# A graph layer on one core: source rows transposed in eight parts of three gathered tiles, between matmul tiles

## The chip, the cores and the metric

The kernel runs on one core of a Trainium2 chip. The metric is the device time of one execution in microseconds (us), and the time before is the median of 11 executions. TensorE (PE) does matrix products into PSUM, VectorE (DVE) and ScalarE (ACT) do elementwise work, GpSimd (POOL) issues the gathers by index, and SyncE (SP) and ScalarE issue the other transfers.

## The reference

There are 12,500 nodes with 32 features and 400,000 edges, sorted by their destination. With `h = max(layernorm(x), 0)`:

```
e_feat = concatenate([h[src], h[dst], edge_attr])     # 96 features per edge
v      = relu(e_feat @ W1 + b1) @ W2 + b2             # 96 -> 64 -> 32
out    = x + maximum(segment_max(v, dst), h)          # per node, over its edges
```

Since the edges are sorted by `dst`, the maximum over a node's edges is a running maximum along the edges. The rows `h[src]` are in random order and have to be fetched one by one.

## The kernel before

**Stripes and chunks.** The edges are cut into 4 stripes (`NS`), which lie on the four groups of 32 partitions, and each stripe into 196 chunks (`NCH`) of 512 edges (`C`). A chunk therefore means 2,048 edges. The main loop (L363) takes two chunks, a *pair*, at a time, so there are 98 pairs.

**Head (L149 to L268).** The layernorm is computed in four pieces of nodes, `h` is written to DRAM for the gathers (`h_d`) and split into two parts for matrix products (`hs`). TensorE projects `h` with the destination part of `W1` in 25 rounds of one transpose and one product (L222 to L231), and the result `q` goes to DRAM. Then the *window stage* (L236 to L268) compares the destinations: each chunk has only a window of at most 32 (`W`) destinations per stripe, so `q` is needed for 32 rows only, and it works out the place in the window where each node's last edge lies (`at`).

**Two ways to the source rows.** Of the 16 blocks of 128 rows (`K`) of a chunk, 12 are fetched by GpSimd: `gather(c)` (L139) issues one indirect transfer per block into the tile `gh` of that chunk, with six such tiles. The other four blocks (`MM`) are looked up by TensorE, as *matmul tiles* (`rows_by_matmul`, L278, a generator that is advanced by `next(tiles)`): seven comparisons per chunk (L285) make one-hot rows `hot`, a product with bfloat16 `others` and 14 products with `hs` (L292, L295) sum up into a PSUM bank `pv`, in which all candidates but the wanted one are pushed far down, and a maximum by VectorE (L297) picks the row into `gm`. The first two chunks and the last have no such tiles.

**A pair.** Both kinds of rows are turned into columns by `to_features` (L321): one transpose over the 12 gathered blocks and one over the four of `gm`, into `ht`. `into_ph` (L375) sums up three products in four PSUM banks `ph`: edge attributes (`ea`), the window of `q` through a mask `of` (VectorE, L370), and the source rows. ScalarE applies the ReLU (`hid`, L389), TensorE multiplies with `W2` into two banks `pv` (L399), VectorE runs the maximum along the edges, started anew at each new destination by `pb` (scan, L404). `leave_1` and `leave_2` transpose the result, pick the last edge of each node with a one-hot `last` (L340, L350), and write the rows to DRAM (`top_d`, L357). Eight matmul tiles are set between these steps.

**What sets the order.** In the loop the orders of SyncE and TensorE are those in which the program is written. Those of VectorE, ScalarE and GpSimd are set by a planner. A gather waits until VectorE has freed a buffer (six chunks back) and for a transfer eight gathers back. `pv` has three PSUM banks, `ph` four, and `tr` one.

**End (L418 to L509).** The two result arrays and `h` are read back, the maxima are taken, `x` is added. A general path (L433) for other inputs is not taken here.

Of the kernel before, what the change touches and what calls it, by code (L numbers as in the profile page):

```python
# [20 lines left out]
DVE = mybir.EngineType.DVE  # L21

# [21 lines left out]
MMC = range(2, NCH - 1)  # L44
AHEAD = 2
PIECE = 2 * A0
ROUND = 12582912.0
# [11 lines left out]
def gnn_kernel(ctx, tc, x, src, src_mm, src_t, dst, dst_next, dst_ext, lo, hi, edge_attr, weights, w1, w2, b2, out):  # L59
# [23 lines left out]
    gathered = ctx.enter_context(tc.tile_pool(name="gathered", bufs=6))  # L83
# [17 lines left out]
    lo_i = const.tile([1, NS, NCH], I32, name="lo_i")  # L101
    nc.sync.dma_start(lo_i, lo.rearrange("(o s) c -> o s c", o=1))
# [6 lines left out]
    node = const.tile([P, NCH], F32, name="node")  # L109
    for s in range(NS):  # L110
        nc.gpsimd.iota(node[s * W:(s + 1) * W], pattern=[[0, NCH]], base=0, channel_multiplier=1,
                       allow_small_or_imprecise_dtypes=True)
# [26 lines left out]
    def gather(c):  # L139
        gh = gathered.tile([P, K, D], F32, name="gh")  # L140
        for k in range(K - MM * (c in MMC)):
            if c * C + k * D < SE:
                nc.gpsimd.indirect_dma_start(  # L143
                    out=gh[:, k, :], out_offset=None, in_=h_d[:, :],
                    in_offset=bass.IndirectOffsetOnAxis(ap=src_i[:, c, k:k + 1], axis=0))
        return gh


    with tc.tile_pool(name="nodes", bufs=1) as pool, tc.tile_pool(name="nodes_ps", bufs=2, space=PSUM) as ps:  # L149
# [4 lines left out]
        sts = [pool.tile([P, 2, PIECE], F32, name=f"st{k}") for k in range(len(pieces))]  # L154
        with tc.manual_schedule(engines={DVE, SP}):
            for st, r in zip(sts, pieces):
                n = r.stop - r.start
                nc.vector.tensor_reduce(st[:, 0, :n], xs[:, r], axis=AX.X, op=ALU.add)
                nc.vector.tensor_scalar(st[:, 0, :n], st[:, 0, :n], 1.0 / D, None, op0=ALU.mult)
                nc.vector.tensor_tensor(h[:, r], xs[:, r], st[:, 0, :n, None].to_broadcast([P, n, D]),  # L160
                                        op=ALU.subtract)
                nc.scalar.activation(sq[:, r], h[:, r], AF.Square)
            for st, r in zip(sts, pieces):
                n = r.stop - r.start
                nc.vector.tensor_reduce(st[:, 1, :n], sq[:, r], axis=AX.X, op=ALU.add)
                nc.vector.tensor_scalar(st[:, 1, :n], st[:, 1, :n], 1.0 / D, EPS, op0=ALU.mult, op1=ALU.add)
                nc.scalar.activation(st[:, 0, :n], st[:, 1, :n], AF.Sqrt)
            for st, r in zip(sts, pieces):
                n = r.stop - r.start
                nc.vector.reciprocal(st[:, 1, :n], st[:, 0, :n])  # L170
                nc.vector.scalar_tensor_tensor(h[:, r], h[:, r], 0.0,
                                               st[:, 1, :n, None].to_broadcast([P, n, D]),
                                               op0=ALU.max, op1=ALU.mult)
                nc.sync.dma_start(h_v[:, r], h[:, r])
# [15 lines left out]


# [3 lines left out]
            for k in range(0, EP // P, EP // P // 4):  # L195
# [5 lines left out]
        iota_a = pool.tile([P, D, A0], F32, name="iota_a")  # L201
        nc.gpsimd.iota(iota_a, pattern=[[0, D], [1, A0]], base=0, channel_multiplier=0,
                       allow_small_or_imprecise_dtypes=True)
        nc.vector.tensor_scalar(others, iota_a, place, -LOW, op0=ALU.not_equal, op1=ALU.mult)
# [7 lines left out]
        lo_w = pool.tile([P, NCH], I32, name="lo_w")  # L212
        nc.scalar.dma_start(lo_w, ap(lo, 0, [[NCH, NS], [0, W], [1, NCH]]))
        nc.vector.tensor_tensor(node, node, lo_w, op=ALU.add)
# [7 lines left out]
        for t in range(0, NT, 4):  # L222
            n = min(4, NT - t)
            hp = ps.tile([P, P], F32, name="hp")
            nc.tensor.transpose(hp[:n * D], h[:, t:t + n].rearrange("p t f -> p (t f)"), ident)
            ht = pool.tile([P, P], F32, name="ht", bufs=2)
            nc.vector.tensor_copy(ht[:n * D], hp[:n * D])
            pp = ps.tile([P, 4, HID], F32, name="pp")
            nc.tensor.matmul(pp[:, :n].rearrange("p t o -> p (t o)"), ht[:n * D],
                             wq[:n * D, :n * HID], start=True, stop=True)  # L230
            nc.scalar.activation(qs[:, t:t + n], pp[:, :n], AF.Copy)  # L231
# [40 lines left out]
    with tc.tile_pool(name="edges", bufs=3) as pool, tc.tile_pool(name="edges_ps", bufs=1, space=PSUM) as ps, \  # L272
            tc.manual_schedule(engines={SP, PE}):
        loaded = {}
        windows = {}
        mm_rows = {}

        def rows_by_matmul():  # L278

            for i, c in enumerate(MMC):  # L280
                kb = pool.tile([P, 2, MM * P], F16, name="kb", bufs=2)
                nc.scalar.dma_start(kb, ap(key_d, i * MM * P, [[0, P], [len(MMC) * MM * P, 2], [1, MM * P]]))
                hot = pool.tile([P, A1, MM * P], F32R, name="hot", bufs=2)
                for k in range(A1):
                    nc.vector.tensor_scalar(hot[:, k], kb[:, 0], key_p[:, k:k + 1], None, op0=ALU.is_equal)  # L285
                its = pool.tile([P, MM * P], BF16, name="its", bufs=2)
                nc.vector.tensor_scalar(its, kb[:, 1], place, None, op0=ALU.is_equal)  # L287
                gm = mm_rows[c] = pool.tile([P, MM, D], F32, name="gm", bufs=6)
                for m in range(MM):
                    e = slice(m * P, (m + 1) * P)  # L290
                    po = ps.tile([P, C], F32, name="pv", bufs=3)[:, :D * A0]
                    nc.tensor.matmul(po, its[:, e], others.rearrange("p f a -> p (f a)"), start=True, stop=False)  # L292
                    for k in range(A1):
                        for part in range(2):
                            nc.tensor.matmul(po, hot[:, k, e], hs[:, part, k].rearrange("p f a -> p (f a)"),  # L295
                                             start=False, stop=(k == A1 - 1 and part == 1))
                    nc.vector.tensor_reduce(gm[:, m, :], po.rearrange("p (f a) -> p f a", a=A0),  # L297
                                            axis=AX.X, op=ALU.max)
                    yield

        def load(c):
            if c % LOAD == 0:
# [5 lines left out]
                for s in range(NS):  # L308
                    g = slice(s * D, (s + 1) * D)
                    nc.scalar.dma_start(db[g, :n], ap(dst_ext, 1 + s * S + c * C, [[0, D], [1, n]]))  # L310
                    nc.scalar.dma_start(pb[g, :n], ap(pen_d, s * S + c * C, [[0, D], [1, n]]))
                for k in range(c, min(c + LOAD, NCH)):
                    loaded[k] = [t[:, (k - c) * C:(k - c + 1) * C] for t in (ea, db, pb)]
            _, base = nc.values_load_multi_w_load_instructions(
                lo_i[0:1, :, c], engines=[SP], min_val=0, max_val=N)
            qw = pool.tile([P, HID], F32, name="qw", bufs=6)
            for s in range(NS):
                nc.sync.dma_start(qw[s * W:(s + 1) * W, :], q_d[bass.ds(base[s], W), :])
            windows[c] = qw, base

        def to_features(c, gh):  # L321
            ht = pool.tile([P, K, D], F32, name="ht", bufs=4)
            n = min(K - MM * (c in MMC), (SE - c * C) // D)
            nc.vector.transpose(ht[:, :n].rearrange("p k e -> p (k e)"), gh[:, :n].rearrange("p k f -> p (k f)"))  # L324
            if c in MMC:
                nc.vector.transpose(ht[:, n:].rearrange("p k e -> p (k e)"),
                                    mm_rows.pop(c).rearrange("p k f -> p (k f)"))
            elif n < K:
                nc.vector.memset(ht[:, n:], 0.0)
            return ht.rearrange("p k e -> p (k e)")  # L330

        def leave_1(c, sm):

            px = ps.tile([P, J, P], F32, name="tr")
            for j in range(J):
# [3 lines left out]
            last = pool.tile([P, J, NS, W], F32, name="last", bufs=2)  # L339
            nc.vector.tensor_tensor(  # L340
                last, iota_w[:, None, None, :].to_broadcast([P, J, NS, W]),
                at[:, :, c * J:(c + 1) * J].rearrange("p s j -> p j s")[:, :, :, None].to_broadcast([P, J, NS, W]),
                op=ALU.is_equal)
            return so, last

        def leave_2(c, so, last):

            pw = ps.tile([P, J, P], F32, name="tr")[:, 0]
            for j in range(J):
                nc.tensor.matmul(pw, last[:, j].rearrange("p s w -> p (s w)"), so[:, j, :],  # L350
                                 start=(j == 0), stop=(j == J - 1))
            wo = pool.tile([P, P], F32, name="wo")
            nc.scalar.activation(wo, pw, AF.Copy)  # L353
            _, base = windows.pop(c)
            for s in range(NS):
                g = slice(s * W, (s + 1) * W)
                nc.sync.dma_start(top_d[s % 2][bass.ds(base[s], W), :], wo[g, s * D:(s + 1) * D])  # L357

        tiles = rows_by_matmul()
# [211 lines left out]
```

## Time and profile before

| | |
|---|---|
| median of 11 executions | 5317.55 us (5302.12 to 5334.65) |
| profiled execution | 5313.9 us |
| its span, first to last instruction | 5312.1 us |
| mean granted TensorE clock | 0.81 |
| TensorE matmuls busy | 3656.1 us, 69% |
| TensorE weight loads busy | 2827.6 us, 53% |
| GpSimd busy | 2233.7 us, 42% |
| VectorE busy | 1846.9 us, 35% |
| ScalarE busy | 315.1 us, 6% |
| gathers (L143) | 2353, of 0.948 us each, with 0.30 us between two |
| matmul tiles | 772 |

The page gives busy times of each engine, then 40 equal slices of the span with a digit for the busy tenths, the granted clock and the transfers. Its rows of waits say which instruction waited for what, with total, number and longest in us. "issue" is time for which the profile shows no cause, "remote" a release that it can't place. In an order of time each line begins with start and length in us; the bracket holds the idle time before, and its releaser. An answer by stretches gives busy us of each engine in each. A matmul of two 32-bit operands appears as two records.

### The profile page before, as it was taken

To read this page: it belongs to the slowest core of one execution; us is meant where nothing else is said; L and a number is where in the kernel's file an instruction comes from. 1 tells how busy PE (TensorE), PEld (TensorE's weight loads), DVE (VectorE), ACT (ScalarE), POOL (GpSimd) and SP (SyncE) were. 2 spreads that over 40 slices of the span, in tenths; PEclk is the share of its full clock that TensorE was granted. 3 is DMA by queue.
4 is the path that set the end of the run, shared out by engine and by line. 5 is a ranking of instruction groups with operands and counts; after the bars stand their busy time and mean duration, and the time that the engine had idled before them with its cause. 6 is when DMAs were issued, how large, how long until landed. Compare 5 with 4: busy or idle time off the path is not lost. (4 is left out here: it accounts for less than half of the span.)

```text
span 5312.1 us, 57318 instructions
## 1 busy us (share of the span) xinstructions
PE 3656.1 (69%) x20281; PEld 2827.6 (53%) x20281; DVE 1846.9 (35%) x3612; ACT 315.1 (6%) x627; POOL 2233.7 (42%) x2369
## 2 busy tenths in 40 slices
PE   2376767676767676767676767676767676767687
PEld 1155555554555555555455555554555565555565
DVE  2333333333323232333333333333333333333344
ACT  1000000000000000000000000000000000000000
POOL 6534343434343434343444344434343434344420
PEclk6588788888888787878887878788888788878788
DMA  3321112111211121112111211121112111211121
GB/s 122 84 61 42 41 38 56 43 41 38 57 42 41 38 57 42 41 38 57 42 42 38 57 42 41 38 57 42 41 40 55 42 41 38 57 42 41 38 54 64
DMA packets 235577, 256.47 MB, mean 48 GB/s; under 512 B 123653, under 2 KB 211861, under 8 KB 222102
## 3 DMA queue, kind: packets, MB, share of 16 engines
q10 hardware_dynamic: 74084, 137.60, 9.6%
q0 software_dynamic: 75296, 38.70, 5.0%
q1 hardware_dynamic: 85906, 76.48, 4.8%
q8 instruction: 159, 2.61, 0.2%
q14 instruction: 132, 1.08, 0.1%
HBM read 238.44 MB, written 14.04 MB: 48 GB/s over the span
## 5 line engine op out<-in xcount | busy, mean ns | idle before, releaser
L143 POOL DMA_INDIRECT gh<-h_d,src_i x2353 | 2229.6, 948 | 2903.3 <-DVE ht L324 2189.4
L295 PE MATMUL pv<-hs,hot 128*128 128x448 f32 x10808 | 2868.9, 419 | 324.5 <-issue 323.8
L295 PEld LDWEIGHTS pv<-hs,hot 128*128 128x128 f32 x10808 | 2336.1, 217 | 1244.5 <-issue 1054.0
L297 DVE TENSOR_REDUCE gm<-pv 128x32 f32<-128x448 f32 x772 | 481.0, 623 | 2348.7 <-remote 1322.4
L292 PE MATMUL pv<-others,its 128*128 128x448 bf16 x772 | 307.5, 398 | 670.6 <-issue 544.1
L350 PE MATMUL tr<-so,last 128*128 128x128 f32 x1568 | 275.5, 287 | 434.0 <-issue 429.2
L285 DVE TENSOR_SCALAR hot<-kb,key_p 128x512 fp32r<-128x512 f16 x1351 | 555.7, 478 | 16.4 <-DMA qw<-q_d 16.4
L404 DVE TENSOR_TENSOR_SCAN sm<-pb,sm,pv 128x512 f32<-128x512 bf16 x195 | 248.6, 1275 | 659.0 <-remote 617.1
L350 PEld LDWEIGHTS tr<-so,last 128*128 128x128 f32 x1568 | 241.1, 201 | 405.3 <-issue 393.1
L292 PEld LDWEIGHTS <-its 128*128 128x128 bf16 x772 | 76.5, 99 | 427.9 <-issue 407.7
L389 ACT ACTIVATE hid<-ph,wt 128x512 f32<-128x512 f32 x392 | 238.7, 690 | 969.8 <-PE ph L379 476.0
L353 ACT ACTIVATE wo<-tr 128x128 f32<-128x128 f32 x196 | 54.5, 278 | 3899.3 <-remote 1213.6
L336 PE MATMUL tr<-ident,sm 128*128 128x128 f32 x784 | 131.3, 294 | 36.0 <-ACT wo L353 35.9
L338 DVE TENSOR_TENSOR so<-tr,wt 128x512 f32<-128x512 f32 x196 | 134.3, 685 | 39.4 <-PE pv L292 25.2
L336 PEld LDWEIGHTS tr<-ident,sm 128*128 128x128 f32 x784 | 104.1, 153 | 73.1 <-ACT wo L353 57.7
L340 DVE TENSOR_TENSOR last<-iota_w,at 128x512 f32<-128x512 f32 x196 | 131.5, 671 | 27.2 <-PE tr L350 27.2
L287 DVE TENSOR_SCALAR its<-kb,place 128x512 bf16<-128x512 f16 x193 | 69.9, 362 | 181.8 <-remote 167.0
L379 PE MATMUL ph<-ht,wt 32*64 32x512 f32 x1568 | 115.7, 614 | 11.4 <-issue 11.4
L324 DVE STREAM_TRANSPOSE ht<-gh 128x384 f32<-128x384 f32 (+1 forms) x196 | 102.8, 563 | 54.8 <-PE ph L379 54.8
L379 PE MATMUL ph<-ea,wt 32*64 32x512 f32 x1568 | 110.1, 617 | 8.7 <-DMA db<-in_dst_ext 8.7
L379 PE MATMUL ph<-of,qw 32*64 32x512 f32 x1568 | 105.5, 592 | 6.6 <-issue 6.6
L399 PE MATMUL pv<-hid,wt 64*32 64x512 f32 x1568 | 108.4, 601 | 0.2 <-ACT hid L389 0.2
(68 smaller groups left out, 396.1 us busy)
## 6 DMA issues: line engine op xcount, KB each, us to landing
ea<-in_edge_attr SPq DMA_DIRECT2D x49, 1024.0 KB
db<-in_dst_ext ACTq DMA_DIRECT2D x196, 256.0 KB
kb<-key_d ACTq DMA_DIRECT2D x193, 256.0 KB
gh<-h_d,src_i POOLq DMA_INDIRECT x2353
pb<-pen_d ACTq DMA_DIRECT2D x196, 128.0 KB
qw<-q_d SPq DMA_DIRECT2D x784, 8.0 KB
top_d<-wo SPq DMA_DIRECT2D x784, 4.0 KB
top_d<-zero ACTq DMA_DIRECT2D x2, 1568.0 KB
```

What stands on the lines that cost most here:

```text
L143: nc.gpsimd.indirect_dma_start(out=gh[:, k, :], out_offset=None, in_=h_d[:, :], in_offset=bass.IndirectOffsetOnAxis(ap=src_i[:, c, k:k + 1 ...
L285: nc.vector.tensor_scalar(hot[:, k], kb[:, 0], key_p[:, k:k + 1], None, op0=ALU.is_equal)
L292: nc.tensor.matmul(po, its[:, e], others.rearrange("p f a -> p (f a)"), start=True, stop=False)
L295: nc.tensor.matmul(po, hot[:, k, e], hs[:, part, k].rearrange("p f a -> p (f a)"), start=False, stop=(k == A1 - 1 and part == 1))
L297: nc.vector.tensor_reduce(gm[:, m, :], po.rearrange("p (f a) -> p f a", a=A0), axis=AX.X, op=ALU.max)
L336: nc.tensor.transpose(px[:, j, :], sm[:, j * P:(j + 1) * P], ident)
L338: nc.vector.tensor_tensor(so, px, b2r[:, None, :].to_broadcast([P, J, P]), op=ALU.add)
L340: nc.vector.tensor_tensor(last, iota_w[:, None, None, :].to_broadcast([P, J, NS, W]), at[:, :, c * J:(c + 1) * J].rearrange("p s j -> p j ...
L350: nc.tensor.matmul(pw, last[:, j].rearrange("p s w -> p (s w)"), so[:, j, :], start=(j == 0), stop=(j == J - 1))
L379: nc.tensor.matmul(ph[s][x * HID:(x + 1) * HID], w[g], e[g], start=start, stop=stop)
L389: nc.scalar.activation(hid[s], ph[s], AF.Relu, bias=b1c)
L404: nc.vector.tensor_tensor_scan(sm, loaded.pop(c + x)[2], pv[x], before, op0=ALU.add, op1=ALU.max)
```

## The change

The source rows of a pair are now transposed one pair ahead, in eight parts. `gather` fills tiles of three blocks (`SOME`), with 24 such buffers instead of six of whole chunks. `to_features(c, part)` transposes one of them right behind the matmul tile of the same number, so that one iteration transposes the eight parts of the *next* pair while it finishes its own.

The orders of VectorE and ScalarE in the loop are written out by hand too. The one-hot comparisons and the `last` masks are placed between the tiles. The mask `of` moves from VectorE (one comparison) to ScalarE (two activations, `window_hots`). All chunks but the last have matmul tiles; those of the first two stand ahead of the loop. Windows and edge data are loaded four chunks ahead instead of two. Keys come for two chunks in one transfer, `db` and `pb` for all stripes in one. The edge and window products of the next pair are issued in this iteration. `pv` has two banks; the freed one holds the numbers 0 to 31 (`iota_ps`) for the `last` masks. `leave_2` uses products of 64 columns instead of 128.

In the head, one of the four pieces of the layernorm goes to GpSimd, some small operations are merged, and the projection works on four transposes and two products at a time. In the end, `h` is put together from `hs` by GpSimd instead of being read from DRAM.

```diff
-MMC = range(2, NCH - 1)
-AHEAD = 2
+MMC = range(NCH - 1)
+SOME = 3
+AHEAD = 4
...
-    gathered = ctx.enter_context(tc.tile_pool(name="gathered", bufs=6))
+    gathered = ctx.enter_context(tc.tile_pool(name="gathered", bufs=24))
...
     def gather(c):
-        gh = gathered.tile([P, K, D], F32, name="gh")
-        for k in range(K - MM * (c in MMC)):
-            if c * C + k * D < SE:
+        n = min(K - MM * (c in MMC), (SE - c * C) // D)
+        parts = []
+        for k in range(0, n, SOME):
+            parts.append(gathered.tile([P, SOME, D], F32, name="gh"))
+            for i in range(min(SOME, n - k)):
                 nc.gpsimd.indirect_dma_start(
...
-        for t in range(0, NT, 4):
+        for t in range(0, NT, 16):
+            fours = [(k, min(4, NT - k)) for k in range(t, min(t + 16, NT), 4)]
...
-            tc.manual_schedule(engines={SP, PE}):
+            tc.manual_schedule(engines={SP, PE, DVE, ACT}):
...
+        iota_ps = ps.tile([P, C], F32, name="iota_ps")[:, :W]
+        nc.vector.tensor_copy(iota_ps, iota_w)
...
-                    po = ps.tile([P, C], F32, name="pv", bufs=3)[:, :D * A0]
+            po = ps.tile([P, C], F32, name="pv", bufs=2)[:, :D * A0]
...
+        def window_hots(c):
+            of = ofs[c] = pool.tile([P, C], F32, name="of", bufs=3)
+            nc.scalar.activation(of, loaded[c][1], AF.Square, bias=below[:, c:c + 1])
+            nc.scalar.activation(of, of, AF.Relu, bias=ones, scale=-1.0)
+
+        def to_features(c, part):
...
+            if part < J:
+                r = slice(part * SOME, min((part + 1) * SOME, n))
+                if r.start < n:
+                    nc.vector.transpose(ht[:, r].rearrange("p k e -> p (k e)"),
+                                        gh[c][part][:, :r.stop - r.start].rearrange("p k f -> p (k f)"))
+            elif c in MMC:
...
+                for g in range(2):
+                    nc.tensor.matmul(pw[g * 2 * W:(g + 1) * 2 * W],
+                                     last[:, j, 2 * g:2 * g + 2].rearrange("p s w -> p (s w)"),
+                                     so[:, j, g * 2 * D:(g + 1) * 2 * D], start=(j == 0), stop=(j == J - 1))
...
         for c in range(0, NCH, 2):
+            a, b = c + 2, c + 3
+            for k in range(a, min(a + 2, NCH)):
+                gh[k] = gather(k)
+            load_keys(a + 2)
             for k in range(c + AHEAD, min(c + AHEAD + 2, NCH)):
                 load(k)
...
+            tile(a, 0)
+            to_features(a, 0)
+            ht = [hts.pop(c + x).rearrange("p k e -> p (k e)") for x in range(2)]
+            into_ph(ph, [(w1a, ht[x]) for x in range(2)], False, True)
...
+            one_hots(b, range(3))
+            tile(a, 1)
+            to_features(a, 1)
+            one_hots(b, range(3, A1))
+            last = [lasts(c)]
+            tile(a, 2)
+            to_features(a, 2)
+            ph = edges_into(a)
...
+            windows_into(a, ph)
+            leave()
...
+            tile(a, 3)
+            to_features(a, 3)
+            to_features(a, J)
+            so = leave_1(c, sms[0])
+            last.append(lasts(c + 1))
+            tile(b, 0)
+            to_features(b, 0)
+            one_hots(a + 2, range(4))
+            leave_2(c, so, last[0])
+            tile(b, 1)
+            to_features(b, 1)
+            so = leave_1(c + 1, sms[1])
+            one_hots(a + 2, range(4, A1))
+            tile(b, 2)
+            to_features(b, 2)
+            tile(b, 3)
+            to_features(b, 3)
+            to_features(b, J)
...
-        for r in pieces:
-            nc.sync.dma_start(h[:, r], h_v[:, r])
```

In it, `tile(c, m)` is one matmul tile with its reduction, `one_hots(c, groups)` some of the seven comparisons of a chunk, and `lasts(c)` the mask of last edges.

## The prediction

> **What bounds the kernel now.** I read the page's totals and slices first, then the waits, then a table of stretches, then the order of time within one pair of chunks.
>
> ```profile
> PE 3656.1 (69%) x20281; PEld 2827.6 (53%) x20281; DVE 1846.9 (35%) x3612; ACT 315.1 (6%) x627; POOL 2233.7 (42%) x2369
> PE   2376767676767676767676767676767676767687
> POOL 6534343434343434343444344434343434344420
> PEclk6588788888888787878887878788888788878788
> ```
>
> No engine is busy throughout, yet all slices look alike until the last one and a half, where POOL (the gathers) has ended and PE and its clock rise. The waits name the partners:
>
> ```profile
> POOL gh L143 <- DVE ht L324: 2189.4, 94, 32.9
> DVE gm L297 <- remote: 1322.4, 88, 28.4
> DVE sm L404 <- remote: 617.1, 85, 13.4
> ```
>
> POOL waits once per pair for the big transposes (94 times, some 23 us), then gathers in one burst. VectorE waits some 15 + 7 us per pair for something that the profile can't name ("remote"). By the program it can only be TensorE: both instructions wait on TensorE's semaphore and for no late DMA. Four stretches of one pair each (columns: length, then busy us and count of PE, PEld, DVE, ACT, POOL, then clock, DMA share, GB/s):
>
> ```profile
> 2602.00:2655.00 53.00, 35.56 (x206) 27.86 (x205) 18.42 (x37) 3.26 (x7) 22.69 (x24) 0.82 0.27 70
> 5108.00:5152.00 44.00, 35.31 (x212) 28.70 (x211) 18.30 (x36) 2.98 (x6) 16.08 (x17) 0.92 0.11 22
> 5152.00:5184.00 32.00, 32.00 (x214) 26.10 (x213) 18.14 (x36) 2.98 (x6) 0.00 (x0) 1.00 0.25 70
> ```
>
> This decides my reading. The same work takes 53 us beside 24 gathers, 44 us beside 17, and 32 us beside none (from one first edge matmul at 5153.26 to the next at 5184.42: 31.2 us). So 31.2 us is TensorE's own time and 52.9 us is what it takes (starts at 2612.80, 2665.54, 2718.59). Inside the pair:
>
> ```profile
> 2620.03 0.94 POOL L143 DMA_INDIRECT gh<-h_d,src_i  x1 [23.37 <-DVE ht L324]
> 2625.55 1.09 PE L399 MATMUL pv<-hid,wt 64*32 64x512 f32 x16
> 2635.73 1.28 DVE L404 TENSOR_TENSOR_SCAN sm<-pb,sm,pv 128x512 f32<-128x512 bf16 x1 [7.84 <-remote]
> 2649.76 0.37 PE L350 MATMUL tr<-so,last 128*128 128x128 f32 x1 [1.73 <-issue]
> 2654.02 0.62 DVE L297 TENSOR_REDUCE gm<-pv 128x32 f32<-128x448 f32 x1 [12.98 <-remote]
> ```
>
> The burst starts at 2620.03 and, at 24 x 1.25 us, ends at 2650.3. The matmuls recorded from 2625.55 to 2626.64 are consumed only at 2635.73; between 2642 and 2653 TensorE issues one instruction per 0.7 or 1.4 us; the reduction of the tile recorded at 2626.6 to 2629.7 starts at 2654.02. A matmul's recorded end cannot be trusted here: the Trainium skill, "Perfetto Trace Analysis", section "Tensor Engine Instruction (MATMUL, LD_WEIGHTS)", says that it is estimated from the size, not observed. So I read completions from who consumes them. In the head, under a burst of 80 gathers, the pace is bare:
>
> ```profile
> 77.27 1.19 PE L229 MATMUL pp<-wt,ht 128*128 128x256 f32 x2 [6.30 <-issue]
> 85.67 1.19 PE L229 MATMUL pp<-wt,ht 128*128 128x256 f32 x2 [7.00 <-issue]
> 94.07 1.19 PE L229 MATMUL pp<-wt,ht 128*128 128x256 f32 x2 [7.00 <-issue]
> ```
>
> 8.40 us a round for three matmul and three load records: 1.40 us an instruction, against 0.11 in a free tile (30 instructions in some 3.3 us). So: a long run of gathers makes TensorE crawl. Onset: the tile before the burst's sixth us is reduced on time (2625.75), so I put it 8.5 us after the start. End: after the last gather, some 1.8 us later (tile issue resumes near 2652).
>
> Here a rule speaks against the change. The Trainium skill, "SBUF — State Buffer", section "SBUF: two separate sides", says that only the port pair shared by VectorE and GpSimd contends and that TensorE never waits on anyone. By it the 21.7 us per pair would not come from gathers, spreading them would be worth nothing, and only head and end would gain: about 5312 - 110 = 5200 us. The 53/44/32 rows say otherwise, and I go by them; what the shared path is, no row here shows.
>
> **The change, part by part.**
>
> Gathers. The number per chunk stays 12 (16 in the first two before), each with the same transfer of 128 rows. Before, two transposes free two buffers together and POOL runs 24 gathers in one go. After, each of eight transposes per pair frees a three-gather buffer, behind its own matmul tile; 24 buffers are again three pairs ahead, so landing stays hidden. Three gathers are 3.75 us; TensorE's starts of tiles in a free pair are 4.2, 3.0, 6.9 (four small groups between), 3.7, 3.9, 3.7, 3.0, 3.0 us apart, sum 31.3. So at TensorE's own pace POOL, with 30.0 us, would hardly ever pause, and the crawl would still begin; but the crawl now stops the releases, and POOL runs dry after at most a few gathers. The pair finds its own period. I take a filling store: it fills in 8.5 us of gathering, empties in 1.8 us after. If emptying goes on at one rate r and gathers fill at p, then 8.5(p - r) = 1.8r, r = 0.83p, and 24 gathers can pass in 30.0/0.83 = 36.4 us. With 0.6 us for uneven release: **37 us a pair** (estimate). Bounds: 31.2 (never sets in) and 52.9 (no help), and beyond it if it sets in at every group (below).
>
> VectorE. Two transposes of 0.56 us become eight of 96 columns: rows of 384 (0.563) and 128 columns (0.304) give 0.175 + 0.0010 a column, 0.27 each, so +1.05 us; the two compares of L370 (0.44 apart) leave: -0.88. Sum 18.3 us of 37; if that cover is gone, +0.2 us a pair, 16 us in all. Its order is now by hand: behind each reduction stand a transpose, compares, then the scans. Gather time is touched: beside the compares of L285 a gather took 1.24 instead of 0.95 us (198.72 to 203.31); 5.7 us of compares now meet gathers, some five of them, +1.4 us for POOL; within the range's upper part.
>
> ScalarE. Four activations for the window masks (nearest row: hid, 0.690): +2.8 us on 3.0, hidden under 37. They stand ahead of the next window matmuls but follow hid with two tiles (6 us) of cover. If not covered: 270 us. Key loads fall from two to one per pair, db and pb from eight to two per four chunks: some 2 us of queue less, on an idle queue. SyncE issues the same 8 window loads (6.3 us) and 8 stores (7.5 us) plus one register load for two: 14 of 37 us, and the loads start two chunks earlier.
>
> TensorE. The leaving matmuls become eight of 64 columns instead of four of 128, twice the records: between 0.5 and 1.9 us against 0.97 a time; I keep 0.97 (column halves can overlap as in L399, 16 records in 1.02 us); the worst is +1.9 us a pair, 175 us. With two tile banks instead of three, the tile after the scan waits for it: last product, then scan 1.28 us, covered by window (0.99) and leaving matmuls (0.97). Zero; without that cover 1.3 us a pair, 120 us.
>
> Head. Before, the projection rounds crawl until 121, the window stage begins at 131.9 and takes 31.4 us, and the first tile is out only at 232.3. After, projections go in fours: 25 groups at the free pace of 0.84 us (pairs at 37.35, 39.04, 40.72) end at about 43 from 22, near the onset; I allow one crawling round of 24 instructions x 1.4 = 34, so 77. Window stage to about 110, loads behind; the first burst is 72 gathers, 30 to 120. Tiles start at about 125 (bounds 110 and 200). Two chunks more by matmul: 8 tiles x 3.4 = 27. Gathers of the layernorm piece on POOL cost some us before the burst, absorbed there.
>
> End. From the last tile to the end 48.6 us; without reading h again (it lands at 5304.46, last): 45.
>
> Sum: 125 + 27 + 93.5 pairs x 37 (3459) + 3 gather-free pairs x 31.2 (94) + 45 = **3750 us**, against the profiled 5313.9 (span 5312.1); that execution lies 0.07% under the median 5317.55, which I ignore.
>
> **Rivals.** Fixed part 291 us, plus 93.5 times the period.
> - Crawl never sets in: short groups with the 6.9 us tile step clear it. 31.3 to 33 us: 3215 to 3375. For it: the first 8 us of a burst are free. Against: POOL would be 96% busy.
> - Crawl sets in after every third group and ends only when POOL pauses: fast for 11.3 us, then about 4 lost: 31.3 x 15.4/11.3 = 42.7, 4280 us; up to 50 if a cold clock (0.50 in the stalls now) adds.
> - No gain: TensorE loses 0.9 us per gather however they are placed: 52 us, 5150. For it: total gathers are equal. Against: 17 gathers lose 12.8 and 24 lose 21.7, so the first 6 or 7 are free.
> - Slower: the store does not empty in the gaps, and each three-gather group stalls TensorE. Place: between a transpose and the next tile. It decides above (5317 - 291)/93.5 = 53.8, that is 2.8 us a group; at the full 3.75 a group: 61 us, 6000. Against: a stalled TensorE gives POOL no new buffers.
>
> **How the numbers follow.** Chances: 34 to 40 us, my forecast, 0.41 (3470 to 4030); never sets in 0.22; 40 to 50 us 0.24; no gain 0.04; slower 0.09. The 8-in-10 range takes the first rival nearly whole and the second to 47 us: 3240 to 4690. Faster 0.90, same 0.01, slower 0.09, where 0.2% is what a measurement of this kernel can tell.
>
> **What would show it.** Right: pair starts about 37 us apart; gathers in threes with pauses; "remote" waits of the reductions down from 1322 to a few hundred; clock above 0.9; first tiles near 125. Wrong: period 31 with POOL without pause (no store at all); period near 53 with short pauses and crawling TensorE; VectorE or POOL without pause as bound.

## The result, and the profile after

| | before | after |
|---|---|---|
| median | 5318.09 us (31 executions, 5293.62 to 5334.65) | 4112.35 us (8 executions, 4100.2 to 4121.15) |
| profiled execution, span | 5313.9, 5312.1 us | 4126.7, 4124.9 us |
| mean granted TensorE clock | 0.81 | 0.89 |

The ratio is 0.7733, 95% interval 0.7721 to 0.7744. The forecast was 3750 us with a range of 3240 to 4690: the direction and the range held, the number was 362 us too low.

The page of the changed kernel, its totals and three rows of slices:

```profile
PE 3639.4 (88%) x21969; PEld 2509.5 (61%) x21969; DVE 1819.7 (44%) x3999; ACT 590.2 (14%) x1007; POOL 2335.6 (57%) x2377
...
PE   2699898999989998889999998999988989998996
...
POOL 7555565655555555555655556555555555655541
PEclk7789898989898899899898989898899889988998
```

TensorE's digits rise from six and seven tenths to eight and nine, and the clock is up. But this isn't work alone: without a crawl (see the experiments) the page of the same kernel has the same 21,969 matmul records busy for 3039.9 us, 600 us less. GpSimd's busy time is what it was (2336 against 2234 us), now in a span that is 1187 us shorter. The waits (total us, times, longest):

```profile
DVE gm L359 <- remote: 1207.3, 208, 20.3
...
POOL gh L148 <- DVE ht L400: 504.4, 187, 8.4
POOL gh L148 <- DVE ht L403: 481.6, 94, 9.5
```

GpSimd's wait for transposes is down from 2189 to 986 us, in three pieces a pair instead of one (281 in all, 3.5 us in the mean). The releases that the profile can't place stay: 1207 us where I had forecast a few hundred. One pair in order of time (start, length, then the idle time before and its releaser):

```profile
2016.13 1.01 POOL L148 DMA_INDIRECT gh<-h_d,src_i  x1 [3.29 <-DVE ht L400]
...
2027.82 0.95 POOL L148 DMA_INDIRECT gh<-h_d,src_i  x1 [4.31 <-DVE ht L403]
...
2037.89 0.95 POOL L148 DMA_INDIRECT gh<-h_d,src_i  x1 [2.57 <-DVE ht L400]
...
2043.76 0.62 DVE L359 TENSOR_REDUCE gm<-pv 128x32 f32<-128x448 f32 x1 [2.01 <-PE pv L356]
...
2052.07 0.95 POOL L148 DMA_INDIRECT gh<-h_d,src_i  x1 [0.30 <-issue]
...
2055.18 0.62 DVE L359 TENSOR_REDUCE gm<-pv 128x32 f32<-128x448 f32 x1 [9.24 <-remote]
...
2056.26 1.01 POOL L148 DMA_INDIRECT gh<-h_d,src_i  x1 [3.24 <-DVE ht L400]
```

Between the first and the last of these lines lie 40.13 us and 24 gathers: six, a pause of 4.31, six, a pause of 2.57, twelve, a pause of 3.24. In the long run TensorE's tiles come out on time until 2043.76, 5.9 us after its start, and then none for 11.4 us. The next is out 2.2 us after the last gather has ended (2053.02). This is the crawl of the prediction, still there, but cut short by GpSimd running dry. From 300 to 3900 us nearly all runs of gathers are of six (173) or twelve (80). A stretch of this pair, and one after the last gather (length, then busy us and count of PE, PEld, DVE, ACT, POOL, then clock, DMA share, GB/s):

```profile
2016.13:2056.26 40.13, 38.64 (x241) 25.38 (x226) 18.03 (x41) 8.00 (x14) 23.60 (x25) 0.92 0.36 82
4000.00:4032.00 32.00, 32.00 (x232) 25.37 (x231) 17.66 (x40) 5.55 (x10) 0.00 (x0) 1.00 0.32 84
```

From the first to the last edge product of a pair that runs beside gathers (158.05 to 4008.80) there are 95 pairs, 40.5 us each in the mean (by these products they alternate between some 37 and 44 us); the two after them take 30.79 us each. The pair therefore went from 52.9 to 40.5 us, and 95 x 12.4 = 1178 of the 1187 us lie there. Which part of the change saved them no run shows; the trace shows only that one wait of 23 us has become three short ones.

### The profile page after: what moved, and what is told of

Same layout as the page of the kernel before. It is cut to its first block, busy times and chain, and to the rows that moved or that the text cites. A ratio compares the mean times of both kernels' runs of the same rounds, so it can differ in the third digit from the quotient of the medians.

```text
span 4124.9 us, 59504 instructions
## 1 busy us (share of the span) xinstructions
PE 3639.4 (88%) x21969; PEld 2509.5 (61%) x21969; DVE 1819.7 (44%) x3999; ACT 590.2 (14%) x1007; POOL 2335.6 (57%) x2377
## 5 line engine op out<-in xcount | busy, mean ns | idle before, releaser
L356 PE MATMUL pv<-hs,hot 128*128 128x448 f32 x10920 | 2585.0, 385 | 179.1 <-issue 175.5
L356 PEld LDWEIGHTS pv<-hs,hot 128*128 128x128 f32 x10920 | 2101.8, 194 | 473.4 <-issue 325.6
L444 PE MATMUL ph<-ea,wt 32*64 32x512 f32 x1568 | 282.3, 921 | 65.5 <-issue 61.0
L506 PE MATMUL pv<-hid,wt 64*32 64x512 f32 x1568 | 295.3, 932 | 21.7 <-DVE last L410 12.5
L430 PEld LDWEIGHTS tr<-so,last 128*64 128x64 f32 x3136 | 128.6, 153 | 200.8 <-issue 195.8
L400 DVE STREAM_TRANSPOSE ht<-gh 128x96 f32<-128x96 f32 x782 | 209.3, 268 | 0.0
L430 PE MATMUL tr<-so,last 128*64 128x64 f32 x3136 | 165.7, 246 | 44.5 <-issue 41.2
L386 ACT ACTIVATE of<-db,below 128x512 f32<-128x512 int32 x196 | 139.2, 710 | 66.6 <-issue 66.6
L387 ACT ACTIVATE of<-of,ones 128x512 f32<-128x512 f32 x196 | 141.5, 722 | 6.4
L410 DVE TENSOR_TENSOR last<-iota_ps,at 128x512 f32<-128x512 f32 x196 | 133.0, 678 | 0.0
```

The costliest lines, as they stand in the source:

```text
L387: nc.scalar.activation(of, of, AF.Relu, bias=ones, scale=-1.0)
L400: nc.vector.transpose(ht[:, r].rearrange("p k e -> p (k e)"), gh[c][part][:, :r.stop - r.start].rearrange("p k f -> p (k f)"))
L430: nc.tensor.matmul(pw[g * 2 * W:(g + 1) * 2 * W], last[:, j, 2 * g:2 * g + 2].rearrange("p s w -> p (s w)"), so[:, j, g * 2 * D:(g + 1) * ...
L444: nc.tensor.matmul(ph[s][x * HID:(x + 1) * HID], w[g], e[g], start=start, stop=stop)
L506: nc.tensor.matmul(pv[x][s * D:(s + 1) * D], w2x[g], hid[s][g], start=True, stop=True)
```

## The experiments

**A condition that the prediction did not have in view.** The twelve runs fell on four chips. On every one of them the kernel before, run beside, took 3190.0 to 3196.2 us instead of 5294 to 5335. So a time below is compared with about 3193 us, and first comes what the trace of the unchanged kernel shows there.

**The kernel before and the changed kernel, unchanged.**

> The kernel before, unchanged, for its trace on a chip of these experiments. Theory A (gathers alone make TensorE crawl, whatever the chip): 5310 us, pairs 52.9 us apart, the reductions of matmul tiles waiting some 1300 us for a release that the trace can't place. Theory B (the crawl needs a condition of the chip beside the gathers, which this chip lacks): about 3194 us, pairs 31.2 to 31.6 us apart, no such waits, no stretch with 1.4 us a TensorE instruction, though the 24 gathers of a pair still go in one burst of 30 us.

> The changed kernel, as it is. In the last runs the kernel before took 3193.67 us instead of 5318, so there the gathers did not make TensorE crawl. If the crawl belongs to the chip or its condition: where the kernel before takes about 3190 us the change is worth little, POOL's 31.3 us and TensorE's 30.5 us a pair give 3150 to 3300 us; where the kernel before takes about 5318 us, this one takes 4112 us again. If the kernel before had only been placed better by chance in those runs and the gain is the change's own: 0.77 of the time of the kernel before in either case.

Measured: 3195.63 us for the kernel before (one execution), and 3156.8 us for the changed kernel, ratio 0.9884 (0.9855 to 0.9912). First the page, the waits and one pair of the kernel before, each a view of its own:

```profile
PE 3056.2 (96%) x20281; PEld 2469.6 (77%) x20281; DVE 1855.2 (58%) x3612; ACT 316.4 (10%) x627; POOL 2349.4 (74%) x2369
...
POOL 5777777777777777777777777777777777777750
PEclk8699999999999999999999999999999999999997
```

```profile
DVE gm L297 <- PE pv L295: 909.3, 611, 4.1
POOL gh L143 <- issue: 646.2, 2120, 0.3
```

```profile
1006.62:1037.78 31.16, 31.16 (x210) 25.32 (x209) 18.43 (x36) 2.98 (x6) 23.84 (x25) 1.00 0.18 34
```

The totals of the changed kernel, and one of its pairs:

```profile
PE 3039.9 (96%) x21969; PEld 2383.2 (75%) x21969; DVE 1826.2 (58%) x3999; ACT 563.2 (18%) x1007; POOL 2329.9 (74%) x2377
```

```profile
2016.91:2047.77 30.86, 30.86 (x225) 24.21 (x225) 17.80 (x40) 5.54 (x10) 23.54 (x25) 1.00 0.31 67
```

The gathers come 0.30 us apart, as before, and never pause; most take 0.94 us, and the mean is 0.997 instead of 0.948 us. TensorE is busy for all of a pair beside them, at clock 1.00, and no release is unplaced. So gathers alone, 24 in 31 us, don't make TensorE crawl; something that the recorded comparison had and these four chips lack is needed as well. It also turns one reading of mine round. The wait of 23 us per pair for the two big transposes was no property of buffers of whole chunks: with the same buffers and no crawl it is gone. So in the recorded comparison it was the crawl that held the transposes back.

Two candidates for the further condition can be looked at in these traces. A lower granted clock explains too little: the pair of 40.13 us had 0.92, so even if all its work went with the clock, 40.13 x 0.92 = 36.9 us would be left at full clock (an estimate), not 30.86; and from 2044 to 2055 us, while no tile came out, the granted clock was 1.00. The gathers' transfers took no longer either. Their queue in the kernel before, in the recorded comparison and here (packets, 32 for each of 2353 gathers; MB; share of the span of 16 engines):

```profile
q0 software_dynamic: 75296, 38.70, 5.0%
```

```profile
q0 software_dynamic: 75296, 38.70, 9.0%
```

That is 266 us of 5312 and 287 us of 3194.

**No gathers.** Only the first two chunks are gathered, and all others use these rows again.

```diff
+    kept = {}
+
     def gather(c):
-        gh = gathered.tile([P, K, D], F32, name="gh")
+        if c > 1:
+            return kept[c % 2]
+        kept[c] = gh = gathered.tile([P, K, D], F32, name="gh")
```

> Leaves out all gathers but those of the first two chunks, whose rows every later pair uses again, so the values are not the reference's. If the gathers make TensorE crawl: the pair falls from 52.9 us to the 31.2 us seen where none were running; 98 x 31.2 = 3058 us, with head and end 3200 to 3350 us. If the 21.7 us per pair come from the order of the work or from waits between the engines (the gathers only happen to be there): about 5200 to 5300 us.

> The changed kernel with the same left out, so again the values are not the reference's. If the gathers are all that holds it above TensorE's own time: 31 us a pair, 3100 to 3250 us. If its order by hand or its two tile banks cost something of their own (windows of VectorE or ScalarE in the way): a period of 34 to 40 us, 3450 to 4100 us.

Measured: 3176.86 us, ratio 0.9947 (0.9925 to 0.9970) for the kernel before, and 3155.6, ratio 0.9884 (0.9851 to 0.9917), for the changed one. TensorE's own time a pair is thus shown: 31.15 and 30.86 us. Compared with the runs that gather, all gathers together cost 17 us in the kernel before, and nothing that shows in the changed one (3155.6 against 3156.8 us, each from two executions that differ by more than 7).

**A slower stream of gathers.** GpSimd fills 384 columns after each gather.

```diff
                 nc.gpsimd.indirect_dma_start(
...
+                nc.gpsimd.memset(pace, 0.0)
...
-            tc.manual_schedule(engines={SP, PE}):
+            tc.manual_schedule(engines={SP, PE, POOL}):
```

(In the changed kernel POOL is added to its own list.)

> The kernel before with one small fill of 384 columns on GpSimd behind every gather, nothing left out. By its nearest rows (784 columns 0.74 us, 128 columns 0.20 us) a fill takes 0.40 us; up to 0.30 of it can lie in the pause between two gathers, so gathers come every 1.35 to 1.65 us instead of 1.25. By the filling store (it can take a gather per 1.51 us): at 1.51 us or slower TensorE doesn't crawl, a pair takes the 36 to 40 us of GpSimd, 3750 to 4150 us in all, so that slower gathers make a faster kernel; at 1.35 us the crawl comes later in the burst, 46 to 51 us a pair, 4750 to 5200 us. If each gather takes a fixed time from TensorE, or if what counts is that GpSimd is at work at all: 5300 us or more.

> The changed kernel with the same fills, nothing left out. By the filling store: at 1.51 us or slower between gathers no crawl is left, and the pair takes GpSimd's 36 to 40 us, 3750 to 4100 us; at 1.35 us 38 to 40 us a pair, 3900 to 4110 us. If each gather costs TensorE a fixed time, or GpSimd's work as such: 40.3 us a pair plus what the fills add, 4110 to 4500 us.

Measured: 3893.04 us, ratio 1.2194 (1.2158 to 1.2229), and 3818.65 us, ratio 1.1961 (1.1926 to 1.1996). Two lines from the order of time and one of the waits of the paced kernel before:

```profile
2000.02 0.95 POOL L146 DMA_INDIRECT gh<-h_d,src_i  x1 [0.17 <-issue]
2000.96 0.44 POOL L149 MEMSET pace<- 128x384 f32 x1
2001.57 0.95 POOL L146 DMA_INDIRECT gh<-h_d,src_i  x1 [0.16 <-issue]
```

```profile
DVE ht L328 <- DMA gh<-h_d,src_i: 971.1, 98, 17.6
```

A gather comes every 1.55 us instead of 1.25, and VectorE waits for rows to land: GpSimd is the bound. A time between 3800 and 3900 us here says nothing of a filling store, since there was no crawl to relieve. But the runs measure slack. In the kernel before the last gather ends 709.6 us later than without the fills (3801.6 instead of 3092.0), and the span grows by 700.5 us (3194 to 3894). In the changed one it ends 707.1 us later (3768.9 instead of 3061.9), and the span grows by 658.0 us (3159 to 3817). So GpSimd was some 9 us from being the bound before, and is some 49 us from it after.

**All eight transposes together**, behind the first tile of the pair.

```diff
             tile(a, 0)
-            to_features(a, 0)
+            for m in range(MM):
+                to_features(a, m)
+            for m in range(MM):
+                to_features(b, m)
...
             tile(a, 1)
-            to_features(a, 1)
```

(The other six calls are taken out likewise.)

> The changed kernel with only the spreading undone: the eight transposes of a pair stand together behind its first matmul tile, so that GpSimd gathers 24 blocks in one burst again; buffers of three blocks, orders by hand and everything else stay. Where the crawl exists: if the spreading is what gained, 50 to 53 us a pair, 4950 to 5250 us; if the rest of the change gained, about 4112 us. Where it doesn't exist (the kernel before at 3190 us): 3150 to 3350 us either way, as the burst of 30 us fits into the pair of 31 us.

> The changed kernel with all eight transposes of gathered rows behind the first tile of the pair, so that 24 gathers go in one burst, once more, for a chip on which the kernel before takes 5318 us. There, by the prediction (spreading is what saves), 4950 to 5250 us against 4112; if the spreading is worth nothing and another part saves, about 4112. On a chip where the kernel before takes 3194 us: 3160 us, as the first time.

Measured: 3160.6 us, ratio 0.9896 (0.9867 to 0.9924), and on another chip 3159.03, ratio 0.9891 (0.9871 to 0.9911). That is 2 to 4 us above the changed kernel's 3156.8, less than its two executions differ (3153.14 and 3160.46): where nothing crawls, the places of the eight parts are worth nothing that shows. Whether they are what saves where TensorE crawls stays open: neither run met it, and without the crawl GpSimd had no pause that a burst could follow.

**Five matmul tiles, eleven gathers.**

```diff
-MM = 4
+MM = 5
...
-                mm_rows[c] = pool.tile([P, MM, D], F32, name="gm", bufs=6)
+                mm_rows[c] = pool.tile([P, MM, D], F32, name="gm", bufs=4)
...
-                hid.append(pool.tile([P, C], F32, name="hid", bufs=6))
+                hid.append(pool.tile([P, C], F32, name="hid", bufs=4))
...
             to_features(a, 3)
+            tile(a, 4)
             to_features(a, J)
```

(The second chunk of a pair gets its fifth tile likewise. The buffers of `gm` and `hid` are fewer to make room.)

> Five matmul tiles and eleven gathers a chunk instead of four and twelve, in the changed kernel. The disputed cost is that of a tile by itself: at 3.2 us of TensorE each, two more a pair make 30.9 + 6.4 = 37.3 us, 98 pairs plus 133 us of head and end: 3790 us where nothing crawls, with GpSimd waiting (22 x 1.25 = 27.5 us of 37.3). Where TensorE crawls (the kernel before at 5318 us), 22 gathers could pass in 33 us by the filling store of the prediction, so that the pair would be TensorE's 37.3 us, 3900 us and faster than 4112; by the third-group rival two fewer gathers only take two of 24 parts of the 9.5 us lost, 37.3 + 8.7 = 46 us, 4700 us.

Measured: 3792.03 us, ratio 1.1873 (1.1849 to 1.1897), pairs 37.3 us apart. A tile costs 3.22 us of TensorE, and GpSimd now waits (view of waits):

```profile
POOL gh L148 <- DVE ht L400: 1044.6, 539, 4.4
```

With three tiles, by these prices, GpSimd would need at least 26 x 1.25 = 32.5 us a pair, more than the 30.86 that a pair takes now; that wasn't run. By this estimate four and twelve is the best split.

**The leaving matmuls.** Of the 128x128 result of a leaving time only the four diagonal blocks are read, one per stripe. Three edits: in the changed kernel back to 128 columns; on to 32; and 64 columns in the kernel before, alone. (The sizes of `wo` and its slices follow.)

```diff
-            pw = ps.tile([P, J, P], F32, name="tr")[:, 0, :2 * D]
+            pw = ps.tile([P, J, P], F32, name="tr")[:, 0]
...
-                for g in range(2):
-                    nc.tensor.matmul(pw[g * 2 * W:(g + 1) * 2 * W],
-                                     last[:, j, 2 * g:2 * g + 2].rearrange("p s w -> p (s w)"),
-                                     so[:, j, g * 2 * D:(g + 1) * 2 * D], start=(j == 0), stop=(j == J - 1))
+                nc.tensor.matmul(pw, last[:, j].rearrange("p s w -> p (s w)"), so[:, j, :],
+                                 start=(j == 0), stop=(j == J - 1))
...
```

> In the changed kernel the leaving matmuls are again four of 128 columns instead of eight of 64. If these small products are what makes a pair of the changed kernel shorter (30.86 against 31.16 us, where nothing crawls), the time rises by 98 x 0.30 = 29 us, 0.9%, to 3186 us. If both forms cost the same (the prediction's 0.97 us a time), nothing changes: 3157 us.

```diff
-                for g in range(2):
-                    nc.tensor.matmul(pw[g * 2 * W:(g + 1) * 2 * W],
-                                     last[:, j, 2 * g:2 * g + 2].rearrange("p s w -> p (s w)"),
-                                     so[:, j, g * 2 * D:(g + 1) * 2 * D], start=(j == 0), stop=(j == J - 1))
+                for g in range(NS):
+                    nc.tensor.matmul(pw[g * W:(g + 1) * W], last[:, j, g],
+                                     so[:, j, g * D:(g + 1) * D], start=(j == 0), stop=(j == J - 1))
...
```

> The changed kernel with leaving matmuls of 32 columns, one per stripe, sixteen instead of eight. If the four column quarters overlap as the two halves do, a leaving time falls from 0.62 us to 0.4 to 0.5 us and the time by 98 x 2 x 0.17 = 33 us to 3124 us (ratio 0.978 to the kernel before); if TensorE's issue of 32 records sets it, 0.6 to 1.2 us a time, 3157 to 3270 us. Where TensorE crawls at 1.4 us an instruction, 16 more records a time make a crawling pair longer: above 4112 us.

The third edit puts the loop over two halves into the kernel before, the first diff read backwards.

> The kernel before with one part of the change alone: leaving matmuls of 64 columns instead of 128. Where nothing crawls (the kernel before at about 3194 us), TensorE is busy nearly all the time, and the twice two leaving matmuls of a pair cost 0.27 us less each (0.88 to 0.62 us in the traces of e9 and e5). If that is what the change is worth there, the time falls by 98 x 0.54 = 53 us to 3141 us, ratio 0.983, and is below the changed kernel's 3157. If the gain of 37 us comes from the new order and the eight parts, the time stays at 3194 us. Where TensorE crawls (the kernel before at 5318 us), within 1% of it by the prediction's reading.

Measured: 3210.55 us with whole columns, ratio 1.0052 (1.0035 to 1.0068); 3122.02 us with quarters, ratio 0.9778 (0.9762 to 0.9794); and 3208.22 us for halves alone in the kernel before, ratio 1.0050 (1.0033 to 1.0066). In the views of groups these products are, with whole columns, halves (the changed kernel) and quarters (count, then busy us in all, mean ns of one):

```profile
L429 PE MATMUL tr<-so,last 128*128 128x128 f32 x1568 | 217.0, 282 | 3.2 <-DVE so L422 3.2
```

```profile
L430 PE MATMUL tr<-so,last 128*64 128x64 f32 x3136 | 134.8, 228 | 3.3 <-DVE so L422 3.3
```

```profile
L430 PE MATMUL tr<-so,last 128*32 128x32 f32 x6272 | 96.4, 200 | 3.3 <-DVE so L422 3.3
```

Twice the records cost less time. Each is half as wide, and they overlap: 3136 records of 228 ns are 715 us in sum and fill 134.8. A leaving time takes 0.89 to 1.00, 0.62 and 0.39 to 0.52 us, from the first record to the next work. The pair is 31.40, 30.86 and 30.46 us, the whole kernel 54 us faster by halves and 35 more by quarters. Whole columns came out above both expectations: without this part the changed kernel is 0.5% slower than the kernel before where nothing crawls. The new order costs TensorE some 0.25 us a pair (31.40 against 31.15). Of that, 0.18 is seen: edge and window products that follow each other directly take 0.91 and 0.99 us (starts at 2003.53, 2004.44, 2005.43 in the kernel before), and 1.04 each when the products with `W2` stand between them. Half of the leaving times are also longer, 1.00 instead of 0.89 us.

The halves alone missed their expectation: 3208 instead of 3141. Most pairs are as short as expected, 30.73 us, but 28 pairs past the first take 31.1 to 36.4. The longest, in order of time:

```profile
2371.09 0.94 POOL L143 DMA_INDIRECT gh<-h_d,src_i  x1 [0.30 <-issue]
2372.34 0.94 POOL L143 DMA_INDIRECT gh<-h_d,src_i  x1 [0.30 <-issue]
...
2372.89 0.58 DVE L324 STREAM_TRANSPOSE ht<-gh 128x384 f32<-128x384 f32 x1 [8.71 <-DMA gh<-h_d,src_i]
...
2374.04 1.19 PE L401 MATMUL pv<-hid,wt 64*32 64x512 f32 x14 [3.10 <-DVE gm L297]
```

and the gathers in its view of groups (busy us, mean ns, then idle time before and its releasers):

```profile
L143 POOL DMA_INDIRECT gh<-h_d,src_i x2353 | 2362.6, 1004 | 741.9 <-issue 657.7 <-DMA gh<-h_d,src_i 43.6 <-DMA h_d<-h 25.0
```

GpSimd doesn't pause: busy and idle fill the 3104 us up to its last gather, and its idle time is that between two gathers. It had some 9 us of slack and was asked for 53. With a gather every 1.309 us in the mean, 24 take 31.4 us, and that is the mean of the pairs. When GpSimd has fallen behind, VectorE waits 8.7 us at the transpose of a whole chunk for its rows to land, the reductions stand behind it, and TensorE waits 3.1 us for a bank. That the kernel is slower than before, and not only no faster, goes with longer gathers: 1.004 us in the mean instead of 0.997, so that the last one ends at 3109.4 instead of 3092.0 us. In the changed kernel the gathers, at 0.982 us beside VectorE's new order, fit. So of the 1.2% neither part does it alone: the halves free TensorE, and the rest of the change leaves GpSimd the room to follow. Which part of that rest it is wasn't tried; the places of the eight transposes are not it, by the run with all of them together. The quarters take 35 of the 49 us that were left, and are the fastest version there, 2.2% below the kernel before. They weren't run where TensorE crawls.

## Why the prediction was right or wrong

**TensorE's own time, 31.2 us a pair.** Right: 31.15 without gathers, and 31.15 beside them where nothing crawls.

**"A long run of gathers makes TensorE crawl."** This step failed as a general statement and held for the recorded comparison. The 53/44/32 us rows were a true reading of that trace, and the traces after carry on: pairs of 40.5 us beside gathers and 30.8 without. But the same 24 gathers leave TensorE at 31.15 us in the trace from one of the four chips, and the times on the other three are the same. I had weighed the rule of the Trainium skill, "SBUF — State Buffer", section "SBUF: two separate sides", that TensorE never waits on anyone. Its 5200 us was wrong for the recorded comparison by 1088 us. In that other trace the measurement agrees with it: TensorE busy for 31.16 of 31.16 us. What the further condition is, no run here shows. In the traces with a crawl, and only there, there are also releases that the profile can't place; whether that is a cause, a sign or a trait of how these executions were recorded wasn't tried.

**Onset 8.5 us, end 1.8 us.** In the pair shown, the last tile on time is out 5.9 us after the start of the run, and the next one, recorded from 2044.70 to 2047.8, is late, so the onset lies between 5.9 and 10 us; the end comes 2.2 us after the last gather. Both fit.

**The filling store, 37 us a pair.** The term that failed in the sum. Measured are 40.5 us: gathers run for 30.9 of 40.1 us, a duty of 0.77 and not 0.83. The step that failed is to take the 1.8 us of emptying for the whole pause. The three pauses of the pair shown are 4.3, 2.6 and 3.2 us: in the last, the late tile is reduced 2.2 us after the last gather, and GpSimd starts again 1.1 us later still, behind a transpose (2053.02, 2055.18, 2056.26). That is nearer to the rival of the third group (fast, then a stall that ends only when GpSimd pauses), which gave 42.7, though the runs are of six, six and twelve gathers and not of nine. By its period the result belongs to that case, 40 to 50 us, and not to the one that I held likeliest, 34 to 40. With 95 pairs instead of 93.5, it is 3850.75 instead of 3459 us: +392 us.

**Head, 152 us to the first edge product.** 158.05, +6, by two errors that cancel. The first tile starts at 94.65 and not 125, below my bound of 110: the projection ends at 40 without the crawling round that I allowed. The eight tiles then crawl, 63.4 us instead of 27 (94.65 to 158.05; on the chip without a crawl 93.20 to 126.07).

**Rest and end.** The two last pairs and what follows take 116 us where I had 94 + 45, -23. The sum is 3750 + 392 + 6 - 23 = 4125, the span.

**Leaving matmuls, kept at 0.97 us.** Wrong within the bounds of 0.5 to 1.9: 0.62 us. Where TensorE crawls, what this is worth wasn't tried; where it doesn't, it is 54 us and decides the sign.

**Edits costed at nothing.** ScalarE's masks take 0.710 and 0.722 us, 2.9 us a pair against 2.8 forecast, hidden: TensorE is busy for all of 30.86 us. The two banks cost nothing that shows: the whole new order costs 0.25 us a pair with leaving matmuls of whole columns, where 1.3 was the worst for the banks alone. The small transposes take 0.268 us. The gathers took 0.984 instead of 0.948 us, +0.9 us a pair against +1.4.

**The rivals.** "Never sets in" gave 3215 to 3375; on the chip where the changed kernel ran without a crawl it is 3157, lower by the leaving matmuls and a head of 126 instead of 152 us. There, though, it never sets in before either. "No gain" and "slower" didn't occur; slower by 0.5% was one small part away.

**The signs that I named.** Of the five for being right, none came as named: pairs 40.5 instead of 37 us apart, gathers with pauses but in sixes and twelves instead of threes, unplaced waits of 1207 us instead of a few hundred, a clock of 0.89 instead of above 0.9, and the first tile at 94.65 instead of near 125. The direction fits the argument, a crawl cut short by GpSimd running dry. That the time came as near as it did is in part luck: the head's two errors cancel, and the range was wide enough for the rival.

## What to carry to other kernels

A stall read from one trace belongs to that kernel in that condition of the chip: before building on its cause, run the unchanged kernel again elsewhere, for the same 24 gathers took 52.9 and 31.15 us a pair. Where two engines end within 2% of each other, an engine's slack is measured by slowing its own step on purpose (0.30 us per gather here): a saving on the other engine beyond that slack is lost or turns into a loss. And a product of which only the diagonal blocks are read can be split into one small product per block: four times the records took less than half the time.

## What the runs showed of the hardware that was not expected

The kernel before takes 5318 us in one comparison and 3193 us on each of four chips, a factor of 1.67. Its gathers are even longer on the faster side, 0.997 instead of 0.948 us in the mean: there 458 of 2353 take more than 1.05 us, 364 of them beside one of VectorE's one-hot comparisons (L285), and in the recorded comparison 10 do.

In the end of the changed kernel, the sum that puts `h` together on GpSimd falls together with VectorE's maxima. Both in order of time, and then the shortest, median and longest of the four maxima in ns:

```profile
4099.17 11.30 POOL L541 TENSOR_TENSOR h_again<-hs 128x3136 f32<-128x3136 f32 x1 [100.93 <-DMA top_d<-wo]
4104.10 9.87 DVE L549 TENSOR_TENSOR acc<-acc,part 128x896 f32<-128x896 f32 x4 [11.40 <-DMA part<-top_d]
```

```profile
L549 DVE TENSOR_TENSOR acc<-acc,part x4: 612/1079/7327, 4104.1 to 4113.4; 128x896 f32<-128x896 f32 x3, 128x448 f32<-128x448 f32 x1
```

The first maximum starts at 4104.10 and lasts 7.33 us, until 4111.43, 0.95 us after GpSimd's sum has ended at 4110.47. The three others take their usual 1.08 and 0.61 us. In the trace of the changed kernel without a crawl it lasts 7.16 us, again until 0.95 us after the sum. So VectorE waited until GpSimd's instruction had ended, at a cost of some 6 us. Here the rule of the same section of the Trainium skill ("SBUF — State Buffer", "SBUF: two separate sides"), that VectorE and GpSimd share a pair of ports as an exclusive lock and that whichever starts first keeps it for its whole instruction, agrees with the trace.
